# Inverse square roots by Newton steps on VectorE in a four-layer cross-attention kernel

## The chip, the cores and the metric

The kernel runs on one core of a Trainium2 chip as one launch. The metric is the device time of that launch in microseconds (us). All work is in single precision except the last feed-forward network, which multiplies quantized whole numbers in bf16. The engines are named as in the profile: PE (TensorE), with its weight loads as PEld, DVE (VectorE), ACT (ScalarE), POOL (GpSimd) and SP (SyncE, which issues DMAs here).

## The reference

Four layers work on a state x of 4 batches x 256 tokens x 256 features. Each layer adds a cross-attention over a context of 4 x 1601 x 256 (layer 1 replaces it by a decayed scan that boils down to one summary vector per batch, layer 2 attends also to the tokens themselves), and then a feed-forward network: 32 experts of which 8 are chosen (layer 0), 8 experts of which 2 are chosen plus a shared one (layer 1), 4 experts of which one is chosen (layer 2), and a network with weights in -1, 0, 1 and activations rounded to 8 bits (layer 3). In outline:

```python
def _layernorm(x, eps=1e-05):
    return (x - mean(x)) / sqrt(var(x) + eps)

x = x + L0_xattn(_layernorm(x), ctx, mask)   # softmax over 1601 context rows, masked
x = x + L0_ffn(_layernorm(x))
x = x + L1_xattn(_layernorm(x), ctx)         # y = Z + summary; layernorm(y) * gamma + beta
x = x + L1_ffn(_layernorm(x))
x = x + L2_xattn(_layernorm(x), ctx)         # 16 heads of 128, 4 of keys; keys, queries: rms_norm, eps 1e-6
x = x + L2_ffn(_layernorm(x))
x = x + L3_xattn(_layernorm(x), ctx)         # 32 heads of 8; keys, queries: t * rsqrt(mean(t*t) + 1e-6)
x = x + L3_ffn(_layernorm(x))
```

So inverse square roots are taken in three kinds of places: a layernorm in front of every attention and network (and one more inside layer 1's attention), the norms of layer 2's keys and queries, and the norms of layer 3's keys and queries over heads of 8 features.

## The kernel before

The tokens lie on 128 partitions, two blocks to a batch (`q` is 0 or 1). A layernorm of one batch is two pairs of batch-norm statistics and aggregates on DVE, one inverse root on a tile of 128 x 2, and two scalings. The inverse root is `rstd` (lines 79 to 82): a Sqrt on ACT and a reciprocal on DVE. ACT holds the tables of one set of functions at a time, and the profile shows an ACT_TABLE_LOAD in front of an instruction that needs another set; Sqrt and the softmax's Exp are in different ones.

The program runs through these stages, in us from the start of the span:

- 0 to 130, layer 0's attention (`l0_xattn`, lines 142 to 344). It begins with the statistics of all batches, those of batch 0 first (its `rstd` at 4.7), those of batches 1 to 3, the opening's later tokens, with one `rstd` over six columns at 15.6. Then, for each batch and block of tokens: scores for all 1601 context rows into four PSUM banks, a DVE pass that adds the mask and takes the maximum (line 261, first at 17.45), Exp (line 271), transposes and the product with the context.
- 130 to 207, layer 0's routing, 207 to 370 its experts, 370 to 505 the gathering of their results together with layer 1's attention (`l1_xattn`, lines 1192 to 1204), which takes two layernorms per batch, one of them behind the other. `normed` (line 115) makes the network's inputs: a layernorm per batch, transposed.
- 505 to 640, layer 1's network.
- 640 to 1735, layer 2's attention, 16 units of 64 us, in which PE is busy almost all the time. `turned(b)` (line 1334) takes one layernorm per batch, `prep` one `rstd` per unit (line 1437). `exps_next` (line 1352) is a small Exp whose table is loaded ahead of the softmax's. Layer 2's keys from the context are not made here but earlier: `l2_early` (line 1206) is a generator that PE's idle stretches in the first three stages take steps from. A step is a block's product, two copies, and now and then squares, sums and a `norm` (lines 1262 to 1267) of 128 x 13 sums, 16 of them, after which POOL scales the keys and PE transposes them.
- 1735 to 1910, layer 2's network, with the keys and values of layer 3's batch 0 beside it (`l3_kv`, line 1671, the filler of this stage).
- 1910 to 1942, the start of layer 3: layer 2's results are gathered (`l2_add`, line 1150), `norms([0])`, the queries of batch 0, with steps of the next batch's keys as fill.
- 1942 to 2541, layer 3's attention. For each batch eight groups of heads are run, and within each seven pairs of context blocks: scores `s` on PE, Exp `e` on ACT (line 1943), products `o` on PE. A pair takes about 2.2 us. `beside` (line 1973) is a generator of side work that gives one step to each pair: the next batch's keys and values, its queries, and the last network for the batch before. The side work on PE goes through one bank of PSUM (`bank()`), which DVE empties (keys and values with three copies per block, lines 1683 and 1685).
- 2541 to 2569, the tail: `norms([3])` and the network of batch 3, nothing else beside them.

In `l3_kv` before the change the squares of the keys are made and summed after blocks 5, 10 and 13 (`l3_squares`, on ACT or POOL, the sum on DVE, line 1724). The inverse roots of all 416 columns come later: for batch 0 by `rstd`, for the other batches within `queries` (lines 1780 to 1826), where one Sqrt over 482 columns (line 1810) covers keys, queries and the variances of the batch whose network is next (`old`), so that ACT changes its table only once there and back. Then POOL scales the keys in four pieces (line 1701).

The order in each engine's queue is worked out at build time from a cost model: among the instructions whose inputs it thinks ready it takes them in program order, so that independent chains are threaded into each other; a few instructions are pinned to program order. Table loads are put in after that.

Of the kernel before, what the change touches and what calls it, by code (L numbers as in the profile page):

```python
# [23 lines left out]
P = 128  # L24
# [5 lines left out]
NM = 13  # L30
# [28 lines left out]
class Kernel:  # L59
# [19 lines left out]
    def rstd(self, out, in_, scale, eps):  # L79

        self.nc.scalar.activation(out, in_, AF.Sqrt, bias=eps, scale=scale)
        self.nc.vector.reciprocal(out, out)

    def layernorm(self, out, x):

        nc = self.nc
        st = self.small.tile([P, 2, 6], F32, name="ln_st")
        mv = self.small.tile([P, 2, 2], F32, name="ln_mv")
        rs = self.small.tile([P, 2], F32, name="ln_rs")
        for q in range(2):  # L90
            nc.vector.bn_stats(st[:, q, :], x[:, q, :])
            nc.vector.bn_aggr(mv[:, q, :], st[:, q, :])
        self.rstd(rs, mv[:, :, 1], 1.0, self.eps5)
        for q in range(2):
            nc.vector.tensor_scalar(
                out[:, q, :], x[:, q, :], mv[:, q, 0:1], rs[:, q : q + 1],
                ALU.subtract, ALU.mult,
            )
# [67 lines left out]
    def l0_xattn(self):  # L166
        nc, tc, i = self.nc, self.tc, self.i
        with ExitStack() as es:
# [142 lines left out]
            for b0, b1 in ((0, 1), (1, B)):  # L311
                for b in range(b0, b1):
                    for q in range(2):
                        st = self.small.tile([P, 6], F32, name="st0")
                        self.pin(nc.vector.bn_stats(st, self.x[b][:, q, :]))
                        self.pin(nc.vector.bn_aggr(mv[:, b, q, :], st))
                self.rstd(rs[:, b0:b1], mv[:, b0:b1, :, 1], 1.0, self.eps5)
                if b0 == 0:
                    xT = turned(0)
# [886 lines left out]
    def l2_early(self, ctxT):  # L1206
# [55 lines left out]
        def norm(kr, ss):  # L1262
            self.rstd(ss, ss, 1.0 / HD2, self.eps6)
            for m in range(0, NM, 4):
# [403 lines left out]
    def l3_kv(self, b, st, early):  # L1668
# [6 lines left out]
        va = st["va"] = self.va3[b % 2]  # L1675
        ss = st["ss"] = self.a3.tile([P, (NM + 2) * NH3 + 2], F32, name="ss3")
        for m in range(NM):
# [11 lines left out]
            if m in (4, 9, NM - 1):  # L1689
                m0 = {4: 0, 9: 5}.get(m, 10)  # L1690
                self.l3_squares(st, kr[:, m0 : m + 1, :], m0, early())
            if m == NM - 1 and b < B - 1:
                self.ctx3 = self.load_ctxT(self.a3, b + 1, 1)
            yield
        if b == 0:
            nk = NM * NH3
            self.rstd(ss[:, :nk], ss[:, :nk], 1.0 / HD3, self.eps6)
        for m0, m1 in ((0, 4), (4, 8), (8, 12), (12, NM)):
            v = kr[:, m0:m1, :].rearrange("p m (h d) -> p (m h) d", d=HD3)
            f = ss[:, m0 * NH3 : m1 * NH3, None].to_broadcast([P, (m1 - m0) * NH3, HD3])  # L1700
            nc.gpsimd.tensor_tensor(v, v, f, ALU.mult)
        yield
# [13 lines left out]
    def l3_squares(self, st, v, m0, early, pool=None):  # L1716
# [5 lines left out]
        else:  # L1722
# [3 lines left out]
            AX.X, ALU.add,  # L1726
        )

    def l3(self, first):
# [11 lines left out]
        with ExitStack() as es:  # L1741
# [30 lines left out]
            def norms(bs):  # L1772

                for b in bs:
                    stats(b)
                v = slice(bs[0], bs[-1] + 1)
                self.rstd(rs[:, v, :], mv[:, v, :, 1], 1.0, self.eps5)

            def queries(b, st, old=None, fill=lambda n: None):

                ss = st["ss"]
                nk, nq = NM * NH3, (NM + 2) * NH3
                if old is not None:
                    stats(old)
                    nc.vector.tensor_scalar(
                        ss[:, nq:], mv[:, old, :, 1], float(HD3), HD3 * (1e-5 - 1e-6), ALU.mult, ALU.add
                    )
                elif b:  # L1790
                    nc.vector.memset(ss[:, nq:], 1.0)
                xn = normed(b, rs[:, b, :])
# [14 lines left out]
                nc.vector.tensor_copy(qr, tq)  # L1807
                self.l3_squares(st, qr, NM, True, one)
                part = ss if b else ss[:, nk:nq]
                nc.scalar.activation(part, part, AF.Sqrt, bias=self.eps6, scale=1.0 / HD3)  # L1810
                nc.vector.reciprocal(ss[:, nk : nq + 2 if b else nq], ss[:, nk : nq + 2 if b else nq])
                qrv = qr.rearrange("p q (h d) -> p (q h) d", d=HD3)
                nc.vector.tensor_tensor(qrv, qrv, ss[:, nk:nq, None].to_broadcast([P, 2 * NH3, HD3]), ALU.mult)
                if b:
                    for c in range(0, nk, nk // 2):
                        nc.vector.reciprocal(ss[:, c : c + nk // 2], ss[:, c : c + nk // 2])
                fill(2)
# [154 lines left out]
            def beside(b, st):  # L1972

                if b + 1 < B:
# [19 lines left out]
                    old = [normed(b - 1, st["ss"][:, nq:])] if b else []  # L1994
                else:
# [18 lines left out]
            norms([0])  # L2014
            for _ in queries(0, first, None, lambda n: [next(kv) for _ in range(FIRST3[n])]):
                pass
# [210 lines left out]
```

## Time and profile before

| | us |
|---|---|
| median of 3 runs | 2565.55 (2564.33 to 2566.97) |
| the profiled execution | 2571.23 |
| its span | 2569.2 |
| PE busy in it | 2429.6 (95%) |
| DVE busy | 1404.4 (55%) |
| ACT busy | 1310.9 (51%) |
| POOL busy | 837.8 (33%) |
| mean granted clock of PE | 0.973 of full speed |

The profile is one execution, and its span begins and ends 2.0 us inside that execution's time. A busy PE need not be a fast one: the granted clock says at what share of its full speed it ran. In a line of the profile an operation is named by its line in the kernel, its engine, and the tiles that it writes and reads.

### The profile page before, as it was taken

Reading aid. Unit: us, or ns where it says so; the run is one execution under the profiler, and the core shown is the slowest. Engines: PE = TensorE matmul, PEld = TensorE weight load, DVE = VectorE, ACT = ScalarE, POOL = GpSimd, SP = SyncE. Lnnn points to the kernel's source line nnn. Section 1 sums busy time; section 2 is a strip of 40 time slices with the busy share of each in tenths; the row PEclk is TensorE's granted clock in tenths of the full one; section 3 lists DMA queues with packets and bytes.
Section 4 is the critical chain, followed back from the end, with each engine's and each line's share of the span. In section 5 each row is a group of like instructions: output and inputs, shape, how many; then the busy total and the mean of one; then the engine's idle time right before and its main releaser. Section 6 shows DMA issues by size and latency. Waiting matters only on the chain.

```text
span 2569.2 us, 47086 instructions
## 1 busy us (share of the span) xinstructions
PE 2429.6 (95%) x17607; PEld 1507.7 (59%) x17623; DVE 1404.4 (55%) x2915; ACT 1310.9 (51%) x3000; POOL 837.8 (33%) x1516
## 2 busy tenths in 40 slices
PE   8989987899989999999999999998999999999997
PEld 5777865777645555555555555565554544544553
DVE  5453534843567777777777777763324324334323
ACT  3234434533654545454545454423336766757875
POOL 1015644213345555555555555541011001011000
PEclk9999998989999999999999999998999999999998
DMA  7165574624601111111111111004310100000000
GB/s 252 49 211 163 169 151 146 216 91 138 225 18 48 48 48 48 47 47 48 47 48 48 47 48 48 9 1 176 125 56 28 35 1 28 6 1 2 6 6 5
DMA packets 96474, 188.45 MB, mean 73 GB/s; under 512 B 15401, under 2 KB 64297, under 8 KB 95050
## 3 DMA queue, kind: packets, MB, share of 16 engines
q1 hardware_dynamic: 80102, 146.50, 16.7%
q0 software_dynamic: 10416, 28.46, 4.6%
q10 hardware_dynamic: 5732, 10.49, 1.3%
q8 instruction: 143, 2.34, 0.4%
q14 instruction: 81, 0.66, 0.1%
HBM read 137.29 MB, written 48.11 MB: 72 GB/s over the span
## 4 chain that ended last, share of the span: by engine, by line
PE 84%; DVE 5%; ACT 3%; DMA 3%; issue 2%; POOL 1%; another core or an unknown queue 1%; SPq 0%; ACTq 0%; PEld 0%; POOLq 0%; DVEq 0%; PEldq 0%
PE s L77 25%; PE o L77 24%; PE fill L1241 3%; PE f2gu L77 3%; PE b L77 3%; PE f1gu L77 2%; PE acc L77 2%; PE tpq L77 2%; PE f0gu L77 2%; PE filly L1241 2%; PE tpkv L77 2%; PE av L77 2%; PE f0y L77 2%; PE f2y L77 1%; PE f1y L77 1%
## 5 line engine op out<-in xcount | busy, mean ns | idle before, releaser
L1487 ACT ACTIVATE p<-s,nmsm 128x448 f32<-128x448 f32 (+1 forms) x512 | 326.1, 643 | 381.4 <-PE s L77 247.5
L1943 ACT ACTIVATE e<-s 128x1024 f32<-128x1024 f32 (+1 forms) x448 | 404.2, 960 | 159.6 <-PE s L77 154.5
L77 PE MATMUL o<-pT,va 128*128 128x256 f32 (+2 forms) x1920 | 434.2, 379 | 9.4 <-DVE pT L1528 7.9
L77 PE MATMUL s<-kT,qT 128*32 128x448 f32 (+1 forms) x4096 | 427.3, 558 | 11.6 <-ACT kT L1459 8.2
L77 PEld LDWEIGHTS o<-pT,va 128*128 128x128 f32 (+1 forms) x1920 | 347.5, 192 | 130.4 <-issue 89.6
L1522 POOL TENSOR_SCALAR p<-p,rm 128x448 f32<-128x448 f32 (+1 forms) x512 | 323.1, 651 | 6.2
L1483 DVE TENSOR_REDUCE nmsm<-s 128x2 f32<-128x896 f32 (+1 forms) x256 | 287.5, 1123 | 7.9
L77 PE MATMUL s<-qb,kT 32*128 32x256 f32 (+1 forms) x3328 | 268.2, 405 | 13.2 <-ACT e L1943 11.0
L1528 DVE STREAM_TRANSPOSE pT<-p 128x896 f32<-128x896 f32 (+1 forms) x256 | 270.7, 1111 | 9.4 <-POOL p L1522 8.7
L77 PEld LDWEIGHTS s<-kT,qT 128*32 128x32 f32 x4096 | 120.2, 110 | 264.0 <-issue 239.0
L77 PE MATMUL o<-e,va 128*32 128x256 f32 (+1 forms) x3328 | 236.3, 392 | 1.2 <-DVE os L2040 1.2
L77 PEld LDWEIGHTS s<-qb,kT 32*128 32x128 f32 (+1 forms) x3328 | 163.4, 181 | 105.2 <-issue 75.5
L1515 POOL TENSOR_TENSOR rm<-em,tot 32x8 f32<-32x8 f32 x256 | 54.2, 212 | 400.8 <-DVE tot L1512 389.6
L1241 PE MATMUL fill<-wkc_early,ctxT 128*128 128x256 f32 (+1 forms) x572 | 146.2, 407 | 13.4 <-ACT kT_early L1277 12.6
L77 PEld LDWEIGHTS o<-e,va 128*32 128x32 f32 (+1 forms) x3328 | 90.6, 110 | 115.1 <-issue 75.0
L1970 POOL TENSOR_TENSOR x<-x,t 128x32 f32<-128x32 f32 x64 | 14.7, 251 | 439.7 <-DVE t L1965 439.7
L1480 DVE TENSOR_TENSOR s<-s,mask 128x128 f32<-128x128 f32 (+1 forms) x256 | 84.3, 330 | 104.7 <-PE s L77 92.5
L1241 PEld LDWEIGHTS fill<-wkc_early,ctxT 128*128 128x128 f32 (+1 forms) x572 | 114.4, 203 | 35.4 <-ACT kT_early L1277 14.8
L458 POOL DMA_INDIRECT f0xr<-f0xd,f0src x95 | 90.5, 953 | 70.6 <-PE f0tph L515 18.7
L1487 ACT ACTIVATION_READ_ACCUMULATOR p<-s,nmsm 128x1 f32 x512 | 101.4, 198 | 0.0
L77 PE MATMUL f2gu<-f2wgu,f2xsT 128*128 x176 | 85.5, 611 | 0.6 <-ACT f2xsT L74 0.3
L566 POOL DMA_INDIRECT f0yt<-f0yd,f0slot x64 | 62.3, 974 | 64.1 <-DVE x L558 33.4
(488 smaller groups left out, 3500.4 us busy)
## 6 DMA issues: line engine op xcount, KB each, us to landing
ctxT<-in_ctxT SPq DMA_DIRECT2D x9, 1664.0 KB
vd<-va_early SPq DMA_DIRECT2D x96, 128.0 KB
kd<-kT_early SPq DMA_DIRECT2D x48, 256.0 KB
kT<-kd SPq DMA_DIRECT2D x16, 768.0 KB
va<-vd SPq DMA_DIRECT2D x16, 768.0 KB
f0yd<-f0ys SPq DMA_DIRECT2D x95, 128.0 KB
wq<-in_l_wq SPq DMA_DIRECT2D x16, 512.0 KB
wo<-in_l_wo SPq DMA_DIRECT2D x16, 512.0 KB
```

The source lines that it names most:

```text
L77: self.nc.tensor.matmul(out, lhsT, rhs, start=start, stop=stop, **kw)
L458: nc.gpsimd.indirect_dma_start(out=t, out_offset=None, in_=xd[:, :], in_offset=bass.IndirectOffsetOnAxis(ap=src[:, n : n + 1], axis=0),)
L566: nc.gpsimd.indirect_dma_start(out=yt, out_offset=None, in_=yd[:, :], in_offset=bass.IndirectOffsetOnAxis(ap=slot[:, t, r : r + 1], axis=0),)
L1241: ins = nc.tensor.matmul(tp[:rows, t, :], ctxT[u // NKV2][:, k, c0 : c0 + rows], w[u % NKV2][:, k, :], start=k == 0, stop=k == 1,)
L1480: nc.vector.tensor_tensor(sv, sv, mask[:, 2 * c : 2 * c + 2, : nt - CT, :].rearrange("p n t i -> p n (t i)"), ALU.add)
L1483: nc.vector.tensor_reduce(ms[:, 0, 2 * c : 2 * c + 2], s[:, :, : nt * 32], AX.X, ALU.max, negate=True)
L1487: nc.scalar.activation(p[:, n, : nt * 32], s[:, n, : nt * 32], AF.Exp, bias=ms[:, 0, e : e + 1], accum_out=ms[:, 1, e : e + 1],)
L1515: nc.gpsimd.tensor_tensor(r[32 * a : 32 * a + 32], e[:, a], tot, ALU.mult)
L1522: nc.gpsimd.tensor_scalar(p[:, n, : nt * 32], p[:, n, : nt * 32], r[:, e : e + 1], 1.0, ALU.mult, ALU.mult)
L1528: self.pin(nc.vector.transpose(pT[:, 2 * c : 2 * c + 2, :nt, :].rearrange("p n t i -> p n (t i)"), p[:, :, : nt * 32]))
L1943: nc.scalar.activation(e[:kr, :, :n, :], s[t][:kr, :, :n, :], AF.Exp, scale=1.0 / math.sqrt(HD3))
L1970: nc.gpsimd.tensor_tensor(xt, xt, t[:, q], ALU.add)
```

## The change

A new method `root` computes the inverse square root on DVE alone: v = scale·x + eps, a first guess from the bits of v (shift right by one, subtracted from a constant), and three Newton steps of three instructions each. That is 12 instructions, each of which reads what the one before it wrote. It takes the place of `rstd` in every layernorm, for batches 1 to 3 in the opening (one root per batch), and in the norm of the early keys. In layer 3 it takes the place of all Sqrts: each part of the keys gets its root and its POOL scaling directly after its squares; the queries get one over 64 columns; the batch for the next network gets its own `norms` call. `prep`'s `rstd` in layer 2 and the one of batch 0 in the opening stay. In `beside` the four steps of the queries now follow one another, after one more step of the keys, where the last two of them came at the end.

```diff
+    def root(self, out, in_, scale, eps, space=None):
+        vec = self.nc.vector
+        n = in_.shape[1]
+        if space is not None:
+            space = space.rearrange("p m d -> p (m d)")
+            v, y, t = (space[:, k * n : (k + 1) * n] for k in range(3))
+        else:
+            v, y, t = (self.small.tile([P, n], F32, name=f"root_{a}{n}", bufs=2) for a in "vyt")
+        vec.tensor_scalar(v, in_, scale, eps, ALU.mult, ALU.add)
+        yi = y.bitcast(I32)
+        vec.tensor_scalar(yi, v.bitcast(I32), 1, None, ALU.arith_shift_right)
+        vec.tensor_scalar(yi, yi, -1.0, float(0x5F3759DF), ALU.mult, ALU.add)
+        for k in range(3):
+            vec.scalar_tensor_tensor(t, y, -0.5, y, ALU.mult, ALU.mult)
+            vec.tensor_tensor(t, t, v, ALU.mult)
+            vec.scalar_tensor_tensor(out if k == 2 else y, t, 1.5, y, ALU.add, ALU.mult)
...
 layernorm:
-        self.rstd(rs, mv[:, :, 1], 1.0, self.eps5)
+        self.root(rs, mv[:, :, 1], 1.0, 1e-5)
...
 l0_xattn:
-                self.rstd(rs[:, b0:b1], mv[:, b0:b1, :, 1], 1.0, self.eps5)
+                if b0:
+                    for b in range(b0, b1):
+                        self.root(rs[:, b], mv[:, b, :, 1], 1.0, 1e-5)
+                else:
+                    self.rstd(rs[:, :1], mv[:, :1, :, 1], 1.0, self.eps5)
...
 l2_early, norm:
-            self.rstd(ss, ss, 1.0 / HD2, self.eps6)
+            self.root(ss, ss, 1.0 / HD2, 1e-6)
...
 l3_kv, after blocks 5, 10 and 13:
-                self.l3_squares(st, kr[:, m0 : m + 1, :], m0, early())
+                sq = self.l3_squares(st, kr[:, m0 : m + 1, :], m0, early())
+                part = ss[:, m0 * NH3 : (m + 1) * NH3]
+                self.root(part, part, 1.0 / HD3, 1e-6, sq)
+                v = kr[:, m0 : m + 1, :].rearrange("p m (h d) -> p (m h) d", d=HD3)
+                nc.gpsimd.tensor_tensor(
+                    v, v, part[:, :, None].to_broadcast([P, (m + 1 - m0) * NH3, HD3]), ALU.mult
+                )
...
-        if b == 0:
-            nk = NM * NH3
-            self.rstd(ss[:, :nk], ss[:, :nk], 1.0 / HD3, self.eps6)
-        for m0, m1 in ((0, 4), (4, 8), (8, 12), (12, NM)):
-            v = kr[:, m0:m1, :].rearrange("p m (h d) -> p (m h) d", d=HD3)
-            f = ss[:, m0 * NH3 : m1 * NH3, None].to_broadcast([P, (m1 - m0) * NH3, HD3])
-            nc.gpsimd.tensor_tensor(v, v, f, ALU.mult)
...
 l3, norms:
-                self.rstd(rs[:, v, :], mv[:, v, :, 1], 1.0, self.eps5)
+                for b in bs:
+                    self.root(rs[:, b, :], mv[:, b, :, 1], 1.0, 1e-5)
...
 l3, queries (the variances of the batch `old` leave ss):
-                self.l3_squares(st, qr, NM, True, one)
-                part = ss if b else ss[:, nk:nq]
-                nc.scalar.activation(part, part, AF.Sqrt, bias=self.eps6, scale=1.0 / HD3)
-                nc.vector.reciprocal(ss[:, nk : nq + 2 if b else nq], ss[:, nk : nq + 2 if b else nq])
+                sq = self.l3_squares(st, qr, NM, True, one)
+                self.root(ss[:, nk:nq], ss[:, nk:nq], 1.0 / HD3, 1e-6, sq)
...
-                if b:
-                    for c in range(0, nk, nk // 2):
-                        nc.vector.reciprocal(ss[:, c : c + nk // 2], ss[:, c : c + nk // 2])
...
 l3, beside:
-                    qs = queries(b + 1, st, b - 1 if b else None)
-                    for _ in range(2):
-                        next(qs)
+                    next(kv)
+                    yield
+                    for _ in queries(b + 1, st):
                         yield
                     for _ in kv:
                         yield
-                    for _ in qs:
-                        yield
-                    nq = (NM + 2) * NH3
-                    old = [normed(b - 1, st["ss"][:, nq:])] if b else []
+                    if b:
+                        norms([b - 1])
+                    old = [normed(b - 1, rs[:, b - 1, :])] if b else []
```

More of the change, by code (lines that the diff above doesn't have):

```diff
@@ L1675, in l3_kv @@
         va = st["va"] = self.va3[b % 2]
-        ss = st["ss"] = self.a3.tile([P, (NM + 2) * NH3 + 2], F32, name="ss3")
+        ss = st["ss"] = self.a3.tile([P, (NM + 2) * NH3], F32, name="ss3")
         for m in range(NM):
@@ L1727, in l3_squares @@
         )
+        return sq
     def l3(self, first):
@@ L1775, in norms, with queries @@
                     stats(b)
-                v = slice(bs[0], bs[-1] + 1)
-                self.rstd(rs[:, v, :], mv[:, v, :, 1], 1.0, self.eps5)
-            def queries(b, st, old=None, fill=lambda n: None):
+                for b in bs:
+                    self.root(rs[:, b, :], mv[:, b, :, 1], 1.0, 1e-5)
+            def queries(b, st, fill=lambda n: None):
                 ss = st["ss"]
                 nk, nq = NM * NH3, (NM + 2) * NH3
[L1785 to L1791, printed above, removed]
                 xn = normed(b, rs[:, b, :])
@@ L2014, in l3 @@
             norms([0])
-            for _ in queries(0, first, None, lambda n: [next(kv) for _ in range(FIRST3[n])]):
+            for _ in queries(0, first, lambda n: [next(kv) for _ in range(FIRST3[n])]):
                 pass
```

## The prediction

> **What bounds the kernel now.** I read the page first, then the table loads in the groups of ScalarE (ACT), then who waits for whom on TensorE (PE) in layer 3, then the timeline of one stall. The page, its busy time and its chain:
>
> ```profile
> PE 2429.6 (95%) x17607; PEld 1507.7 (59%) x17623; DVE 1404.4 (55%) x2915; ACT 1310.9 (51%) x3000; POOL 837.8 (33%) x1516
> PE 84%; DVE 5%; ACT 3%; DMA 3%; issue 2%; POOL 1%; another core or an unknown queue 1%; SPq 0%; ACTq 0%; PEld 0%; POOLq 0%; DVEq 0%; PEldq 0%
> ```
>
> PE is the bound: only about 140 of 2569.2 us are without a matmul, and a change that adds no matmul can win only there and in the time that PE runs at half clock. The groups of ACT:
>
> ```profile
> L81 ACT ACT_TABLE_LOAD x34 | 43.6, 1283 | 2.6 <-DVE ln_st L91 1.9
> ...
> L1352 ACT ACT_TABLE_LOAD x17 | 21.8, 1283 | 0.3
> ...
> L1943 ACT ACT_TABLE_LOAD x6 | 7.7, 1283 | 0.1
> ...
> L1810 ACT ACT_TABLE_LOAD x3 | 3.8, 1283 | 1.6 <-DVE ss L1724 1.6
> ```
>
> Each Sqrt among the Exps costs a load of 1283 ns there and one back. Sixteen of the pairs L81/L1352 belong to `prep`'s `rstd` of layer 2, which stays. Which loads PE feels, the waits in the window from 1900 to 2569 us tell (total, times, longest):
>
> ```profile
> PE s L77 <- ACT e L1943: 11.0, 4, 3.4
> PE w L1908 <- DVE hb L1904: 7.2, 1, 7.2
> PE w L1879 <- DVE xb L1872: 6.0, 2, 5.3
> PE b L77 <- DVE va L1685: 2.6, 3, 1.9
> PE fill L77 <- ACT va L1685: 2.1, 1, 2.1
> ```
>
> One of the four stalls behind `e`, in the timeline:
>
> ```profile
> 2146.93 0.69 DVE L1724 TENSOR_REDUCE ss<-sqq 128x64 f32<-128x512 f32 x1 [0.70 <-ACT sqq L1721]
> ...
> 2147.70 1.28 ACT L1810 ACT_TABLE_LOAD   x1 [0.80 <-DVE ss L1724]
> 2148.99 0.70 ACT L1810 ACTIVATE ss<-ss,eps 128x482 f32<-128x482 f32 x1
> 2149.71 1.28 ACT L1943 ACT_TABLE_LOAD   x1
> ...
> 2151.00 2.86 ACT L1943 ACTIVATE e<-s 128x1024 f32<-128x1024 f32 x3
> ...
> 2152.08 2.08 PE L77 MATMUL s<-qb,kT 32*128 32x256 f32 x8 [3.43 <-ACT e L1943]
> ```
>
> ACT makes no softmax weights from 2147.70 to 2151.00, PE waits 3.43, and then runs slowly. The windows of the stretch (length; busy PE, PEld, DVE, ACT, POOL; then the granted clock):
>
> ```profile
> 2151.50:2158.50 7.00, 6.42 (x48) 2.68 (x48) 7.00 (x12) 4.45 (x6) 6.73 (x4) 0.51 0.01 2
> 2158.50:2170.00 11.50, 11.50 (x161) 6.73 (x158) 5.21 (x19) 7.77 (x9) 0.50 (x3) 1.00 0.01 1
> ```
>
> 7.0 us at 0.51 of the clock lose 7.0×0.49 = 3.4, so the stall costs 3.4+3.4 = 6.8 us. The spacing of the `e` instructions checks this: seven pairs with nothing beside them take 15.42, those with one more step each about 19.26, and this head took 25.90, which is 6.6 more; its twin at 2316 took 6.5 more.
>
> **Price of a root.** It is 12 dependent DVE instructions (3 TENSOR_SCALAR, 6 SCALAR_TENSOR_TENSOR, 3 TENSOR_TENSOR). Dependent small ones in the opening start at 19.76, 19.93 and 20.11, so 0.17 to 0.18 each; in a busy queue I allow 0.19, and a two-column root is 12×0.19 = 2.3 us. What it replaces in the tail ran from 2543.46 (end of the aggregates) to 2544.02 (xn), 0.56 with its table already loaded. So an exposed small root adds 1.7. A two-input row grows from 0.22 at 64 columns to 0.69 at 512, 1.05 ns a column, so 64 columns take 12×0.25 = 3.0, 96 take 3.5, 160 take 4.3. Where DVE has independent work it is threaded between: at 2545.52 a RECIPROCAL of 0.15 is followed by another instruction after 0.07. The Trainium skill ("VectorE: DVE Perf Modes", section "The DRAIN you can't avoid") says the next instruction waits until the pipe is empty and tells authors to keep their number down; by it each root would hold DVE for its whole 2.3 to 4.3 us, whatever stands beside it, and (a) below would go to its upper bound, 17 us more.
>
> **Layer 3, what goes.** The queries' Sqrt leaves ACT (loads L1810 and L1943), three times: two heads of 6.6 and 6.5. The load pair of `norms([2])` at 2414.5, with a PE wait of 1.50, made its head 2.0 longer. Together −15.1. At the first head the same things (loads at 1944.2, 1947.2, 1957.7, 1959.7) and DVE's jam made 26.25 out of 21.0, which is 5.2. There the three later roots add 36 instructions to DVE in the same jam, which I price at 2 of those 5.2. Before it, L81's load holds ACT from 1919.6 to 1925.1, and the filling matmuls wait 2.07; but x arrives by DMA only at 1924.8, so that after it a root of 2.3 instead of 0.6 gives most of it back. With the first queries' root (3.0 for a Sqrt and a reciprocal that took 1.1) I take −3.0 for the whole start (bounds −7 and +3). The Trainium skill ("ScalarE: Activation LUTs", "What ACT_TABLE_LOAD costs") gives 2.66 us for a switch with its drain; the trace has 2.60 for both switches of a query (3.30 held, 0.70 Sqrt), and by the page three queries would free 8 us more of ACT.
>
> **Layer 3, what comes.** (a) Keys' roots of 160, 160 and 96 columns now run on DVE at the 5th, 10th and 13th block instead of two reciprocals of 1.4. Seven fall among the heads: one for batch 1, three each for batches 2 and 3. They stand in DVE's queue with the next block's copies out of the only side bank and with `os`. The reduce alone (1.49) makes PE wait 0.37 at 2108.97 and 0.36 at 2273.2. Bounds 0 (threaded between) and 2.9; I take 0.5, near that row: +3.5. (b) POOL's four scalings (6.8 us a batch) become three, spread out; while they ran, DVE's xn at 2156.72 took 1.34 against 0.40 alone, so they may hold a copy by a us, but before they held others: 0. On POOL the next squares come five blocks, some 11 us, behind a scaling of 2.3; no DMA moves. (c) The four query steps now follow one another. From tq at 2145.5 qr, square, reduce, root and product take 0.7+0.7+0.7+3.0+0.7 = 5.8, and the transposes stand two pairs later, 4.4. PE could wait 1.4; the planner may put scores first. 0 to 1.6, taken 0.6, three times: +1.8. (d) `norms([b-1])` apart from the queries is 12 small instructions in a DVE that is 194.6 of 599 us busy: 0. Layer 3: −15.1−3.0+3.5+1.8 = −12.8.
>
> **The rest.** Tail: `norms([3])` is on DVE's chain with PE waiting: +1.7. End of layer-1 attention: y, z and the first `normed` go through three roots in turn between 505.9 and 515.3 with DVE dense and PE waiting 2.01 behind xn; three times 1.7 exposed would be 5.1 plus clock, while the loads at 521.8 and 523.6 go (a wait of 0.78). Bounds +1 and +9, taken +4. Opening: three roots of 36 instructions stand before the first mask-and-max at 17.45 instead of a 0.5 chain; 36×0.1 = 3.6, of which the statistics' gaps take some: 0 to +4, taken +1.5. Layer 0's routing: the last layernorm's root, +0.8 (0 to +3). Layer 2's entry loses the L1487 load (PE waits 2.99 at 711.9) but now needs its Sqrt load at 685.5: −0.5 (±3). The early keys' 16 norms, the layer-2 `turned` roots and layer 2's FFN have slack (layer 2: PE 1068.7, DVE 808.8 of 1095; kr_early waits on POOL for its transposes much later): 0 (−1 to +3). Sum 1.7+4+1.5+0.8−0.5 = +7.5.
>
> **Total.** −12.8+7.5 = −5.3. The profiled execution took 2571.23 (span 2569.2 and 2.0 around it), so 2565.9; it lies 5.7 above the median of 2565.55, so the median becomes 2560.3.
>
> **Rivals.** *Full gain* (0.24): roots are threaded everywhere, (a), (c), opening and layer 1 cost a third: −12.8−3.5+2.5 = −13.8, 2551.7. For it: DVE is a third busy in layer 3. Against: the chains at 510 and 2543 have nothing to thread with. *A wash* (0.14): layer 1 and opening at their upper ends (+7.5 more than taken), 2567.8; this differs from the last rival in place. *DVE becomes late in layer 3* (0.21, slower): the root stands whole in front of the next block's copies, 1.49+4.3 = 5.8 us against a pair of 2.2. PE then waits, and from 1.25 us the wait costs the clock too (the wait of 1.25 at 2021.5 was followed by 0.57 until 2025.5): 1.25+1.7 = 2.95 a time, seven times 20.6 instead of 3.5: 2577.4; at half of the seven, 2569. It decides from the point where a copy stands over 2 us behind a root. The Trainium skill ("TensorE: Matmul & The Clock Gate", Part 1) has the clock fall after an idle window of about 3.4 us; by it these waits would cost 1.25 each, 2565.5, but 1.25 and 2.07 sufficed here. *No effect* (0.04): another wait stood behind the loads and takes their place, 2565.6; the 6.6 us of two heads speak against it. My forecast has 0.37.
>
> **How the numbers follow.** From no change a measurement can tell about 0.2%, 5.1 us. Forecast and full gain are mostly over it: faster 0.50. Full gain 0.24 and 0.7 of the forecast's 0.37 make 0.50; half the wash, the case of no effect and most of the rest of the forecast 0.19; the slower rival with the wash's other half and what is left 0.31. The range runs from full gain with layer 1 free (2548) to the slower rival at most of its seven (2575); the forecast and the full gain alone would have 2549 to 2566.
>
> **What would show it.** Right: no table load after 1960 us save the tail's, heads of about 19 to 21 us where 25.9 stood, the wait of `s` for `e` from 11.0 to under 2, L81 loads from 34 to about 18, a PE gap near 515 of 5 to 6, tail longer by 1.7. Wrong: waits of `b` for va or `o` for `os` over 1.25 after blocks 5, 10 and 13 with a clock near 0.5 behind them, or a first softmax after 20 us.

## The result and the profile after

The changed kernel takes 2608.11 us (2602.46 to 2612.8, 5 runs) where the kernel before takes 2565.55: 42.6 us more, a ratio of 1.0161 (95% interval 1.0143 to 1.0178). The profiled execution took 2612.8 us, its span is 2611.1, so the two spans differ by 41.9. In the new listing the copies in `l3_kv` are 23 lines lower down (L1685 is now L1708), later lines by less; the Exp of layer 3 is L1952, and the root's instructions are L94 to L101. The page's busy time and its chain:

```profile
PE 2437.4 (93%) x17623; PEld 1509.9 (58%) x17623; DVE 1513.5 (58%) x3660; ACT 1249.1 (48%) x2911; POOL 838.2 (32%) x1512
PE 81%; DVE 10%; issue 3%; DMA 2%; ACT 2%; POOL 1%; another core or an unknown queue 1%; SPq 0%; ACTq 0%; DVEq 0%; POOLq 0%
```

PE's work is nearly the same, and DVE's share of the chain has doubled from 5% to 10%. The loads did what was forecast. In the groups of ACT (L1375 is `exps_next`, L1352 before):

```profile
L1375 ACT ACT_TABLE_LOAD x17 | 21.8, 1283 | 0.3
L81 ACT ACT_TABLE_LOAD x16 | 20.5, 1283 | 0.3
...
L1952 ACT ACT_TABLE_LOAD x1 | 1.3, 1283 | 0.0
```

L81 went from 34 loads to the 16 of layer 2's `prep`, the Exp of layer 3 from 6 to 1, and L1810's three are gone. Yet the waits of PE from 1945 us to the end (in all, times, longest) have a new first line:

```profile
PE b L77 <- DVE va L1708: 20.9, 7, 4.7
PE w L1888 <- DVE xb L1881: 7.8, 2, 7.2
PE w L1917 <- DVE hb L1913: 7.1, 1, 7.1
PE b L1833 <- DVE qr L1825: 5.6, 4, 1.6
...
PE s L77 <- ACT e L1952: 1.4, 1, 1.4
```

The wait for `e` fell from 11.0 to 1.4 as forecast, and a wait for DVE's copies out of the side bank took its place, 2.6 before and 20.9 now. The other large wait stands at the end of layer 1's attention, in the window from 500 to 545 us, where 2.0 stood before:

```profile
PE tp_ln L146 <- DVE xn L114: 14.3, 1, 14.3
```

Where the time went is read by putting the two traces side by side: the same instruction of DVE or ACT (the n-th of its line) starts later in the trace of after by so much, and the growth of that lag from stage to stage is what the stage costs. The stages are named by the times of before.

| stage | growth of the lag, us | forecast |
|---|---|---|
| opening (0 to 30) | +2.2 | +1.5 |
| layer 0, rest (30 to 400) | +1.7 | +0.8 |
| layer 1's attention (400 to 520) | +15.1 | +4 |
| layer 1's network, entry of layer 2 (520 to 760) | +3.2 | −0.5 |
| layer 2's attention (760 to 1720) | 0.0 | 0 |
| layer 2's network (1720 to 1880) | −3.7 | 0 |
| start of layer 3 and its first head | +10.5 | −3.0 |
| rest of batch 0 and heads of batches 1 and 2 | +13.1 | −7.8 |
| first head of batch 3 | −2.4 | −2.0 |
| tail | +2.1 | +1.7 |

In layer 3 the unit to read is the head: from the first `e` of one group of heads to the first `e` of the next. Where nothing is changed these times repeat from kernel to kernel, mostly to 0.1 and at most to 0.3 us, and they will judge the experiments. Two exceptions: the first head, and a head with a wait after which the clock falls in one run and not in another (up to 1.7 us, see "Clock" below).

| kernel | first head | batch 1, heads 1 to 3 | batch 2, heads 1 to 3 | batch 3, head 1 |
|---|---|---|---|---|
| before | 26.25 | 25.47, 25.88, 25.90 | 25.86, 25.88, 25.72 | 18.34 |
| after | 33.71 | 29.35, 33.10, 21.54 | 29.74, 33.10, 21.54 | 15.96 |

So the third heads got shorter by 4.2 to 4.4, as the loads left, and the two in front of them longer by 3.9 and 7.2. The timeline of DVE, POOL and PE shows why, behind the tenth block of batch 2's keys:

```profile
2162.82 1.49 DVE L1746 TENSOR_REDUCE ss<-sq 128x160 f32<-128x1280 f32 x1 [2.04 <-POOL sq L1745]
...
2164.34 0.24 DVE L94 TENSOR_SCALAR sq<-ss 128x160 f32<-128x160 f32 x1
...
2167.70 0.32 DVE L100 TENSOR_TENSOR sq<-sq 128x160 f32<-128x160 f32 x1
2167.94 0.42 DVE L1706 COPY kr<-b 128x256 f32<-128x256 f32 x1
...
2168.51 0.48 DVE L1708 COPY va<-b 128x128 f32<-128x128 f32 x2
...
2169.13 3.23 PE L77 MATMUL b<-wkv,ctxT 128*128 128x512 f32 x4 [3.62 <-DVE va L1708]
```

The eleventh block's product had left PE at 2163.9, but the copy that empties the bank starts at 2167.94, behind the sum (1.49) and eleven of the twelve root instructions, 0.28 to 0.36 apart. PE waits 3.62 us for the bank and then takes 3.23 for matmuls that take 1.98 at full clock; the granted clock was 0.58 in the 4 us from 2169. The fifth block's root made a wait of 2.27 in the same head, with the clock at 1.00 behind it. Together 2.27 + 3.62 and about 1.7 of clock (4 us at 0.58) come near the 7.2 by which the head grew. The wait of 2.20 us at 2124.56, in the first head, has no key root in it:

```profile
2118.23 0.17 DVE L94 TENSOR_SCALAR root_v<-mv 128x2 f32<-128x2 f32 x1
...
2120.61 0.73 DVE L1790 TENSOR_SCALAR xn<-x,mv,rs 128x256 f32<-128x256 f32 x2
...
2123.59 0.42 DVE L1706 COPY kr<-b 128x256 f32<-128x256 f32 x1
...
2124.56 3.03 PE L77 MATMUL b<-wkv,ctxT 128*128 128x512 f32 x4 [2.20 <-DVE va L1708]
```

Here the layernorm of the batch whose network comes next, and its rounding to 8 bits, stand in front of the copy. Before the change its variance waited in `ss` for the queries' Sqrt; with a `norms` call of its own it is ready as soon as x is, and the planner (the step that orders the queues at build time) drew it forward to the first pairs, although the program has it at the end.

### The profile page after: what moved, and what is told of

It reads as the page before. It is cut to its first block, busy times and chain, and to the rows that moved or that the text cites. A ratio compares the mean times of both kernels' runs of the same rounds, so it can differ in the third digit from the quotient of the medians.

```text
span 2611.1 us, 47741 instructions
## 1 busy us (share of the span) xinstructions
PE 2437.4 (93%) x17623; PEld 1509.9 (58%) x17623; DVE 1513.5 (58%) x3660; ACT 1249.1 (48%) x2911; POOL 838.2 (32%) x1512
## 3 DMA queue, kind: packets, MB, share of 16 engines
q8 instruction: 143, 2.34, 0.4%
## 4 chain that ended last, share of the span: by engine, by line
PE 81%; DVE 10%; issue 3%; DMA 2%; ACT 2%; POOL 1%; another core or an unknown queue 1%; SPq 0%; ACTq 0%; DVEq 0%; POOLq 0%
PE s L77 24%; PE o L77 23%; PE fill L1264 3%; PE f2gu L77 3%; PE b L77 3%; PE f0gu L77 2%; PE acc L77 2%; PE f1gu L77 2%; PE tpq L77 2%; PE tpkv L77 2%; PE av L77 2%; PE f0y L77 2%; PE f2y L77 1%; PE filly L1264 1%
## 5 line engine op out<-in xcount | busy, mean ns | idle before, releaser
L1952 ACT ACTIVATE e<-s 128x1024 f32<-128x1024 f32 (+1 forms) x448 | 404.0, 959 | 197.1 <-PE s L77 192.0
L481 POOL DMA_INDIRECT f0xr<-f0xd,f0src x95 | 90.5, 953 | 61.5 <-PE f0y L77 23.6
L1283 DVE TENSOR_REDUCE ss_early<-sq_early 128x4 f32<-128x512 f32 x64 | 37.3, 582 | 87.5 <-ACT sq_early L1282 64.5
```

The costliest lines, as they stand in the source:

```text
L481: nc.gpsimd.indirect_dma_start(out=t, out_offset=None, in_=xd[:, :], in_offset=bass.IndirectOffsetOnAxis(ap=src[:, n : n + 1], axis=0),)
L1283: nc.vector.tensor_reduce(ss[:, m0:m1], sq[:, : m1 - m0, :], AX.X, ALU.add)
L1952: nc.scalar.activation(e[:kr, :, :n, :], s[t][:kr, :, :n, :], AF.Exp, scale=1.0 / math.sqrt(HD3))
```

## The experiments

The time before is about 2524 us in all of them; they ran on other chips, and why the first runs took 41 us more wasn't tried. In the traces the difference (45 us between the profiled executions) lies between 200 and 480 us (layer 0's experts and gathering); from 760 to 1720 us they agree to 0.1 us. After itself ran only with the first runs; by its ratio it would be 41 above before here, which is an estimate. So a kernel is compared with the runs of before of its own call, and stages with e3, which is the kernel before up to layer 2's network. Times in the head table below are read as above.

| kernel | us | before | ratio (95% interval) | first head | batch 1, heads 1 to 3 | batch 2, heads 1 to 3 |
|---|---|---|---|---|---|---|
| e1 early keys by Sqrt | 2557.98 | 2524.37 | 1.0139 (1.0122 to 1.0155) | 35.02 | 29.34, 33.10, 21.54 | 29.73, 33.09, 21.54 |
| e2 layernorms by Sqrt | 2541.77 | 2524.37 | 1.0068 (1.0051 to 1.0084) | 34.71 | 29.34, 33.09, 21.54 | 29.74, 33.09, 21.54 |
| e3 layer 3 alone | 2544.39 | 2524.37 | 1.0077 (1.0055 to 1.0098) | 34.71 | 29.35, 33.09, 21.54 | 29.73, 33.10, 21.54 |
| e4 threaded | 2560.32 | 2524.37 | 1.0154 (1.0132 to 1.0177) | 35.84 | 29.40, 32.39, 21.54 | 29.73, 32.26, 21.60 |
| e5 threaded and pinned | 2533.05 | 2523.94 | 1.0033 (1.0021 to 1.0046) | 35.63 | 29.41, 25.88, 23.33 | 28.09, 25.88, 23.33 |
| e6 norm with queries | 2543.31 | 2523.94 | 1.0072 (1.0055 to 1.0089) | 34.72 | 25.47, 33.09, 21.57 | 25.86, 33.11, 21.57 |
| e7 one root in norms | 2544.42 | 2523.94 | 1.0083 (1.0065 to 1.0100) | 32.70 | 29.34, 33.09, 21.54 | 29.72, 33.09, 21.54 |
| e8 late scaling | 2540.33 | 2523.94 | 1.0064 (1.0048 to 1.0081) | 32.86 | 27.70, 34.32, 21.55 | 29.72, 33.01, 21.54 |
| e9 | 2520.39 | 2524.84 | 0.9979 (0.9970 to 0.9989) | 26.28 | 25.47, 25.89, 23.72 | 25.86, 25.88, 23.73 |
| e10 unread roots | 2556.07 | 2524.84 | 1.0132 (1.0117 to 1.0147) | 33.75 | 29.34, 33.09, 21.53 | 29.73, 33.09, 21.54 |
| e11 e9 and early roots | 2516.67 | 2524.84 | 0.9971 (0.9961 to 0.9981) | 26.27 | 25.47, 25.88, 23.70 | 25.86, 25.88, 23.78 |
| e12 e11, last part later | 2517.99 | 2523.57 | 0.9976 (0.9967 to 0.9985) | 27.68 | 25.47, 25.88, 23.93 | 25.86, 25.88, 24.01 |
| e13 e12, last part tied | 2506.17 | 2524.14 | 0.9936 (0.9921 to 0.9950) | 26.28 | 25.47, 25.88, 18.96 | 25.86, 25.88, 18.96 |

**Which roots cost outside layer 3 (e1, e2, e10).** e1 takes the early keys' roots out of the changed kernel, e2 the layernorms'.

```diff
 e1, l2_early, norm:
-            self.root(ss, ss, 1.0 / HD2, 1e-6)
+            self.rstd(ss, ss, 1.0 / HD2, self.eps6)
 e2, layernorm:
-        self.root(rs, mv[:, :, 1], 1.0, 1e-5)
+        self.rstd(rs, mv[:, :, 1], 1.0, self.eps5)
```

> Kernel after, with the norms of the early keys back to Sqrt and reciprocal (16 units of 12 instructions less on VectorE). Theory A (VectorE is full at the end of layer 1's attention, 43.3 of 45 us between 500 and 545, because the early keys' roots and sums crowd in among the layernorm chains, so that the last gather of x comes 12 us late and PE stands 14.3 us): PE's wait for xn near 538 falls to under 5 us and the whole gains 8 to 16 us against after (2608), so 2592 to 2600. Rival B (the layernorms' dependent roots make that wait by themselves): the wait stays above 10 us and the whole gains under 4 us.

> Kernel after, with only the 24 layernorms back to Sqrt and reciprocal; opening, early keys and layer 3 keep their roots. Theory A: the early keys still fill VectorE, the wait near 538 stays above 6 us, the whole gains 3 to 7 us against 2608. Rival B: the wait falls to the 2 us of before, the whole gains 10 to 16 us.

After would be 41 above before on these chips; e1 is 33.6 above, e2 only 17.4. By the lag at the start of layer 1's network, against e3, the front of the kernel costs 15.6 with all roots (read from e4, which is after up to there; 19.0 on the chip of after), 13.1 without the early keys' and 6.2 without the layernorms'. PE's wait for xn is 14.3, 10.7 and 5.0. So the layernorms count for more, 9.4 against 2.5, and neither theory's numbers came: A, which blamed the early keys, wanted e1's wait under 5, and B wanted e1's gain under 4 (it is 7.4) and e2's wait at 2. Such lags are rough: e5 to e9, which are e3 up to there, lie between −1.1 and +3.7 of it. The growth within the stretch alone (370 to 490 us of e3) is steadier, −0.4 to +1.4 in these five, and there all roots cost 14.9, without the early keys' 13.3, without the layernorms' 8.8. The two parts don't add up: the early keys' roots alone (e2, and e11 to e13 below) cost 7.6 to 8.8 in this stretch, while taking them out of the whole saves 1.5. But why do the layernorms cost it, by their chains or by their place on a full DVE? e10 runs the same twelve instructions for each layernorm into a tile that nobody reads, and takes the root itself by Sqrt.

```diff
 e10, layernorm:
-        self.root(rs, mv[:, :, 1], 1.0, 1e-5)
+        self.rstd(rs, mv[:, :, 1], 1.0, self.eps5)
+        self.root(self.small.tile([P, 2], F32, name="idle_rs"), mv[:, :, 1], 1.0, 1e-5)
```

> Kernel after, but each layernorm takes its inverse root by Sqrt and reciprocal, and the twelve root instructions run beside it into a tile that nobody reads: their time on VectorE stays, the wait for them goes. After is about 41 us above before, e2 (no such instructions at all) 17 above. Theory F (VectorE is full at the end of layer 1's attention, so the instructions' time counts): this stays near after, 33 to 41 above before, and PE's wait for xn there stays above 10 us. Rival G (the layernorms' chains are longer by each root, so the wait for it counts): this is like e2, 17 to 22 above before, the wait 5 us.

It is 31.2 above before, between the two theories and nearer to F. Of the 23.6 us between e2 and after, 13.8 stay although nobody waits for these roots. The lag at the start of layer 1's network is 11.8: of the 9.4 that the roots cost there, 5.6 stay and 3.8 go; by the growth within the stretch (12.0) 3.2 of 6.0 stay. PE's named wait, however, falls to 4.6, as in e2. So about half or more of it is DVE's time, and the rest goes with the chain; the split is no finer than the spread of such lags. The windows of the stretch in e10 (length; busy PE, PEld, DVE, ACT, POOL; clock) show how full DVE is:

```profile
420.00:440.00 20.00, 17.46 (x78) 14.47 (x77) 19.36 (x72) 10.16 (x29) 15.43 (x16) 0.91 0.80 267
440.00:460.00 20.00, 16.94 (x88) 13.95 (x86) 19.86 (x85) 11.11 (x32) 5.74 (x6) 1.00 0.63 203
```

**Is layer 3 a matter of its own (e3)?** The kernel before with the layer-3 part of the change alone.

> The kernel before with the layer-3 part of the change alone (layernorms, opening and early keys as before). If the stages are independent, as the shifts of the trace say (+18.5 us up to the start of layer 3, +21 within it, +2 in the tail, of 41.9 in all), this is 21 to 24 us slower than before: 2587 to 2590. If the loss in layer 3 came from the other roots' disturbance of what stands ready at its start (x, the queues), it would be within 8 us of before.

20.0 above before, just under the 21 to 24 expected, and head by head within 0.3 us what after has, but for the first head, which takes 34.7: the loss is made in layer 3 itself.

**Root or POOL's scaling (e4, e5, e8).** e4 gives the keys' roots out in pieces, behind the copies of each further block; e5 also pins them and the copies in DVE's order; e8 leaves the roots and moves the scalings.

```diff
 e4, l3_kv:
+            for _ in range(13 if m in (8, NM - 1) else 4 if m > 9 else 3):
+                next(late, None)          # one root instruction each, the scaling last
             if m in (4, 9, NM - 1):
...
-                self.root(part, part, 1.0 / HD3, 1e-6, sq)
+                late = scaled(m0, m + 1, sq)
 e5, on the layer-3 part alone, as e4 and:
+            keep(copy(kr[:, m, :]...))     # keep: the pin; also on va's copies and each root instruction
 e8, on the layer-3 part alone:
-                nc.gpsimd.tensor_tensor(v, v, part[:, :, None].to_broadcast(...), ALU.mult)
...
+        for m0, m1 in ((0, 4), (4, 8), (8, 12), (12, NM)):
+            ...
+            nc.gpsimd.tensor_tensor(v, v, f, ALU.mult)
```

> Kernel after, with the roots of the keys in layer 3 given out three or four instructions per block of the context (behind that block's copies in program order) in place of all twelve at once; as many instructions as after. Theory C (the root stands whole in front of the next block's copies): the waits of 2.27 and 3.62 us of PE for va behind the 5th and 10th block of batches 2 and 3 fall below 0.6, the heads of 33.1 us become 26 to 28, and the whole gains 10 to 16 us against 2608. Rival D (VectorE is held up by POOL's scalings of 2.4 us, in which small instructions took 1.4 to 2.4 us): the heads stay above 31 us and the whole gains under 5 us.

> The kernel before with the layer-3 part of the change (as in e3_layer3_alone, 20 us slower than before), but the keys' roots given out three or four instructions per block and pinned in VectorE's queue behind the copies of that block, so that the planner can't draw them ahead as it did in e4. As many instructions and POOL scalings as e3. Theory C (the root stands in front of the next block's copies): the waits behind the 5th and 10th block go, the heads of 33.1 us become 26 to 28, twice, and the whole is 5 to 12 us above before. Rival D (POOL's scalings hold VectorE): the heads stay above 31.

> The layer-3 part alone (as e3) with the roots of the keys where the change puts them, but POOL's scalings put back to the end, in four pieces, as before the change. Rival D (VectorE's copies and small instructions are slow while POOL scales, 2.4 us a part): the heads of 33.1 fall below 30 and the first head by over 2. Theory C: the waits of 2.27 and 3.62 us stay, the heads stay above 31.

e4 changed little (33.1 to 32.4), which by its expectation spoke for D. Its timeline shows that it didn't do what it was meant to: eleven of the twelve instructions of the second part still stood before the next block's copy (presumably the planner thinks them ready sooner than the block). With the pins of e5 the second heads are 25.88 in both batches, to the hundredth what they were before the change, with as many instructions and the same scalings; the third heads take 1.8 of the 7.2 back (23.33 for 21.54). The waits of PE from 1930 us on:

```profile
PE b L77 <- DVE va L1725: 4.4, 2, 2.2
PE b L1851 <- DVE qr L1843: 3.2, 2, 1.6
```

Two of the six waits for va are left, those of the first heads. e8 leaves the heads at 33 to 34: POOL's scalings don't make them. So the cost of the two roots of 160 columns in layer 3 is their place, and the place costs 7.2 us in the second head of a batch. e5's first head (35.63) didn't gain: there the pins tied the copies behind the start's jam (the crowd of instructions that start together on DVE there), with one wait of 8.45 us.

**The drawn-forward normalization (e6) and the start (e7).** e6 sends the variances through the queries' root again; e7 takes one root over six columns for batches 1 to 3.

```diff
 e6, queries:
+                    stats(old)
+                    nc.vector.tensor_scalar(ss[:, nq:], mv[:, old, :, 1], float(HD3), ..., ALU.mult, ALU.add)
-                self.root(ss[:, nk:nq], ss[:, nk:nq], 1.0 / HD3, 1e-6, sq)
+                self.root(part, part, 1.0 / HD3, 1e-6, sq)      # 66 columns
 e7, norms:
-                for b in bs:
-                    self.root(rs[:, b, :], mv[:, b, :, 1], 1.0, 1e-5)
+                self.root(rs[:, v, :], mv[:, v, :, 1], 1.0, 1e-5)
```

> The layer-3 part alone (as e3), but the variances of the batch whose network comes next go through the queries' root (66 columns) as before the change, so that its normalization and quantization can't be ready before the queries. Theory E (they are drawn forward to the head's first pairs and stand ahead of a block's copies; wait of 2.2 us near 2124 after the change): the heads of 29.4 and 29.7 us become 25.5 to 26, the heads of 33.1 stay, the whole is 11 to 14 us above before in place of 20. If the waits there have another cause, these heads stay above 28.5.

> The layer-3 part alone (as e3), but norms(1..3) at the start of layer 3 takes one root over six columns in place of three, 24 small instructions fewer. If VectorE's queue there is full of them (the first head takes 34.7 us in e3, 26.2 in before), it falls to 30 to 32.5 and the whole to 16 to 18 us above before; if the keys' roots and the x sums fill it, it stays within 1 us.

e6 brings the first heads back to 25.47 and 25.86, the values of before. Theory E holds. The whole gained less than the 7.8 of the heads, 19.4 above before where 11 to 14 were expected: the fourth heads became 1.4 and 1.1 longer, as the normalization now stands in front of `os`, the copy of a pair's products out of their bank (PE waits 1.32 for it), and the medians of e3 and e6 are each uncertain by some us. e7 shortens the first head by 2.0 to 32.70, just short of the 30 to 32.5 expected, and its median doesn't show it; the 24 instructions are a part of the jam, not the jam.

**A version from these readings (e9, e11, e12, e13).** e9 is the kernel before, with roots for the keys of batch 0 and, in batches 2 and 3, for keys (pinned as in e5) and for queries and variances together (as in e6), with the queries' steps in the order of before, and one for `norms([2])`. The start of layer 3 and batch 1 stay with Sqrt. e11 adds the early keys' roots.

> Built from what the runs showed: the kernel before with roots only where they took a table load off PE's path and VectorE has room. Layernorms, opening, early keys, the start of layer 3 and all of batch 1 in it as before; keys of batch 0 by roots (layer 2's network, 3 us less in e3); in batches 2 and 3 keys' roots threaded and pinned behind the copies (e5), the variances of the next network's batch with the queries' root (e6), the queries' steps in the order of before; norms([2]) by a root. From the heads: 25.9 and 25.7 become 19.3 to 21.6, 18.3 becomes 16.0, and 3 us in layer 2's network: 12 to 18 us faster than before, ratio 0.993 to 0.995. If the loads' stall is only replaced by a wait for the queries' root, under 7.

> As e9_best, with the early keys' norms by roots as well. In e2 these cost 6 us up to layer 1's network and gave 6.5 between 640 and 760 us (the table loads at the entry of layer 2's attention gone): so within 4 us of e9_best. If they only cost once layer 3 is right, 4 to 8 slower than e9_best.

Both beat the kernel before, by 0.21% and 0.29%, but by less than expected: the third heads took 23.7 in place of 19.3 to 21.6, and the fourth became 1.2 and 0.6 longer than before. The early roots alone make no difference that the runs can tell; the lag at 1880 is 5.5 us smaller with them, but such lags differ by as much between e3 and e5 to e8, which have none of them. e9's start of layer 3 and first head are those of before (its lag changes by less than 0.1 us from 1880 to 2080), so the +10.5 comes from what the change does at the start. The new wait of e9:

```profile
2095.84 0.95 DVE L1769 TENSOR_REDUCE ss<-sq 128x96 f32<-128x768 f32 x1 [4.02 <-POOL sq L1768]
2096.71 0.20 DVE L2011 RECIPROCAL r<-b 128x8 f32<-128x8 f32 x1
...
2096.95 0.22 DVE L2013 TENSOR_TENSOR t<-b,r 128x64 f32<-128x64 f32 x1
...
2097.31 0.73 PE L1842 MATMUL b<-ident,xn 128*128 128x128 f32 x4 [3.14 <-DVE sq L102]
```

DVE waits 4.02 us for POOL's last squares, and behind it in the queue stand the reciprocal `r` and the product `t`, which read the side bank and free it (the line names the root instruction `sq` beside them, which ended last). e12 lets POOL scale one block earlier and puts the last part (squares, sum, root and scaling of the last three blocks) two steps later in the program; e13 keeps the first of these and ties the last part behind the first key transposes' copy.

```diff
 e13, l3_kv, with the key transposes:
+                if b >= 2 and m0 == 0 and h == 0:
+                    with self.tc.issue_after(ins):     # ins: the copy just made
+                        sq = self.l3_squares(st, kr[:, 10:NM, :], 10, False)
+                    late = scaled(10, NM, sq)
+                for _ in range(6 if b >= 2 and m0 == 0 else 13):
+                    next(late, None)
```

> As e11_best_early (8 us faster than before). There the heads of 25.9 became 23.7 and not 19.3, with a wait of 3.1 us: the squares of the last three key blocks stood on POOL behind the 2.4 us scaling of the part before, and VectorE, waiting for them in order, kept the bank from the queries' transposes. Here that scaling is issued two blocks earlier and the last part two steps later, behind the queries' root. If that is the cause, the two heads take 19.3 to 21.6 and the whole is 12 to 17 us faster than before, ratio 0.993 to 0.995; if the queries' chain itself holds PE, they stay above 23 and the ratio at 0.997.

> As e12_best2, which did not shorten the heads of 23.7 (23.9): its trace shows PE's wait of 3.4 us for the bank behind the root of the last 96 key columns, which the planner had drawn ahead of the product t that frees the bank. Here that root is tied behind the first key transposes' copy and given out six instructions at a time. If a root in front of what frees the bank is the cause here as with the other two parts, the two heads take 19.3 to 21 us, the waits of 3.1 to 3.4 us go, and the whole is 12 to 18 us faster than before (ratio 0.993 to 0.995). If the queries' root and product are late by themselves, the heads stay above 22.5.

e12 failed: the last sum came earlier (at 2090.48, 4.6 us ahead of the end of PE's wait, 1.5 in e9), but the planner drew eleven of the twelve instructions of the last root in behind it, in front of the bank's release, and PE waited 3.42:

```profile
2090.48 0.95 DVE L1780 TENSOR_REDUCE ss<-sq 128x96 f32<-128x768 f32 x1 [2.48 <-POOL sq L1779]
2091.47 0.21 DVE L99 TENSOR_SCALAR sq<-ss 128x96 f32<-128x96 f32 x1
...
2094.25 0.26 DVE L109 TENSOR_TENSOR sq<-sq 128x96 f32<-128x96 f32 x1
...
2094.72 0.22 DVE L2024 TENSOR_TENSOR t<-b,r 128x64 f32<-128x64 f32 x1
...
2095.08 1.08 PE L1853 MATMUL b<-ident,xn 128*128 128x128 f32 x4 [3.42 <-DVE t L2024]
```

e13 moved that whole part, its sum and root with it, and the heads are 18.96 both; the fourth heads stay 1.3 and 0.7 longer than before. It is 18.0 us faster than before, ratio 0.9936 (0.9921 to 0.9950). Its waits of PE from 1930 us to the tail:

```profile
PE o L77 <- DVE os L2093: 3.0, 3, 1.2
PE b L77 <- DVE sq L99: 0.7, 2, 0.4
```

What was 8.4 for `e` before and 16.2 for va after in batches 1 to 3 is gone, and the roots are still there. The queries' chain, 5.8 us by the forecast, holds nobody in the order of before.

## Why the prediction was wrong

Forecast was −5.3, measured +42.6. By the table above layer 3 missed by 34.4 us (13.5 at its start, 20.9 in the heads) and layer 1's attention by 11.1.

**What held.** The price of a root: two columns took 2.34 us from the first start to the last end (2118.23 to 2120.57; forecast 2.3), 64 columns 3.0 (3.0), 160 columns 4.25 with one copy in it (4.3). The loads: e13's third heads are 6.9 and 6.8 shorter than before, batch 3's first one 2.4, together 16.1 against the 15.1 of the forecast (14.1 with the fourth heads, which grew by 2.0). The tail: +2.1 against 1.7. The opening: +2.2 against 1.5, within its bounds. The wait for the queries' root: 1.59, at its bound of 1.6 and not the 0.6 taken.

**Term (a), keys' roots at 0.5 each, is the step that failed in layer 3.** I argued from a third-busy DVE and from a wait of 0.37 behind the sum alone that the root would be threaded between the copies. The four roots of 160 columns in batches 2 and 3 cost 3.6 each (7.2 a second head). The queue's order is fixed at build time: in the program, too, the root stands in front of the next block's copies, and the planner left it there, presumably since by its model the block's product came later. The rival that made DVE late in layer 3 has the mechanism. It had seven times 1.25 of waiting and 1.7 of clock, 20.6 in all; measured are seven waits of 2.99 on average, 20.9 without the clock, and the six in batches 1 and 2 made their heads 22.2 longer. That 20.6 and 20.9 look alike is an accident. Four of the seven are roots of 160 columns (2.27 and 3.62, twice), two are the normalization of the next network's batch, one of 4.70 is the start's jam, and the 96-column parts made no wait of this kind. The rule of the Trainium skill ("VectorE: DVE Perf Modes", section "The DRAIN you can't avoid") that I set against the row at 2545.52 leads to the better price here, but by luck: the same section says that a next instruction that isn't held starts earlier, and in e5's jam (1903.7 to 1909.4) instructions of several root chains do alternate, as little as 0.07 apart. The row of 0.07 us between starts is right for independent instructions, and it was mine to see that the planner, not the engine, decides which of them come between.

**Term (d), `norms([b-1])` at nothing, was wrong by 3.9 us a batch.** I costed its twelve instructions and not that the change frees the whole normalization and rounding from the wait for the queries. The diff shows it: the variance leaves `ss`. An edit that takes away a wait lets the work behind it start earlier, and here it started in front of a copy that PE needed (e6).

**The start of layer 3, −3.0, came out at +10.5.** I knew of the jam and put 2 us on it. The lag grows by 3.1 before the first `e` and by 7.5 in the first head. The runs split it in part, against e3's first head of 34.7 (e6 has the same): about 2.0 for three roots in place of one (e7), 1.85 for the place of the scalings (e8). The rest, with the key roots, the x sums and the layernorm's and queries' chains, was not taken apart; with the forms of before it is gone (e9).

**Layer 1's attention, +4 with bounds of 1 and 9, came out at +15.1.** I counted three exposed chains at the end and gave the early keys' roots and the other layernorms nothing, "they have slack". DVE was busy 37.2 of the 40 us from 480 to 520 already before, and 24 instructions came in for each batch's two layernorms, 12 for each early unit beside them. e10 shows that about half or more of the layernorms' part is that occupancy. How it divides further among the single layernorms wasn't tried, and the whole of 15.1 was not taken apart beyond e1, e2 and e10. Nor was the +3.2 of the next stage (−0.5 forecast): without the layernorms' roots (e2) that stage is 6.6 shorter than in e3.

**Clock.** The prediction had half clock after waits of 1.25 and 2.07, and priced 1.7 us of it behind every wait from 1.25 on. That threshold doesn't hold: in the same trace of before the clock stayed at 1.00 in the 4 us behind the waits of 1.50 (2418.69) and 1.89 (1947.32). After the change it fell behind the wait of 2.20 at 2124.56, where four matmuls took 3.03 in place of 1.98, and not behind the longer one of 2.27 at 2143.55 (length; busy PE, PEld, DVE, ACT, POOL; clock):

```profile
2124.50:2128.50 4.00, 3.94 (x12) 1.69 (x16) 2.05 (x8) 0.00 (x0) 0.00 (x0) 0.60 0.00 0
2143.50:2148.00 4.50, 4.45 (x42) 2.14 (x44) 2.60 (x10) 1.32 (x2) 2.42 (x1) 1.00 0.02 4
```

In e8 it is the other way round (1.00 behind 2.19, 0.50 behind 2.26), and with it batch 1's first head is 1.65 shorter there than in e3 and its second 1.2 longer. So the length of such a wait alone doesn't tell its cost here. The Trainium skill ("TensorE: Matmul & The Clock Gate", Part 1) asks for an idle window of about 3.4 us; some of the shorter waits here had the cost as well.

## What to carry to other kernels

An instruction that moves to an engine with idle time costs nothing only where its queue puts it behind the work that others wait for: name what stands behind it, above all copies that free a buffer with a single instance, and check the order that the scheduler will make, since it places by its own estimate of readiness. A long dependent chain is best given out in pieces tied behind the copies: here the same two roots cost a head 7.2 us or nothing. And when an edit removes a wait, ask what was held back by it and where that work will now run.

## What the runs showed of the hardware

While POOL scaled the keys, some small DVE instructions lasted until POOL's was done: the masked query `qb` (128 x 256), 0.34 us at other places, took 2.38 at 2168.91 beside a scaling of 2.40 that began at 2168.73, and a root instruction on 128 x 2 values took 2.36 at 1977.01, 0.15 otherwise, beside one of 2.52 that began at 1976.84. I had put this at up to a us. The copies that free the side bank were not held: beside the scaling of 2.42 that began at 2145.24, the copy of the keys took 0.42 at 2145.54 and those of the values 0.28 each, as elsewhere. That fits e8, where the place of the scalings changes the three heads of batches 1 and 2 by 0.4 and 0.1 us in all, the first head by 1.85 and the fifth head of batch 0 by 1.5.
